# Attention and feed-forward on one core: two silu calls moved into the same beat

## The chip, the core and the metric

The kernel runs on one core of a Trainium2 chip. A core has a matrix engine (TensorE, PE in the profile, with its weight loads as PEld), a vector engine (VectorE, DVE), a scalar engine that evaluates functions from tables (ScalarE, ACT), a general engine (GpSimd, POOL), and queues that start transfers (SyncE, SP, and the queue of POOL). Each engine works through its own list of instructions in order and waits on semaphores for the others.

The metric is the device time of one execution in microseconds, as the median of several executions. A profile describes one execution, which has its own time.

## The reference, cut to what matters

A layer of cross-attention is followed by a feed-forward layer with quantized weights and activations. There are 2048 latent tokens of width 256, and 1601 context tokens; keys and values come from both.

```python
x = x + _L0_xattn_ref(ctx_1024, _layernorm(x), mask, ...)   # 4 heads of 64, rmsnorm on q and k, softmax
x = x + _L0_ffn_ref(_layernorm(x), w1, conv_w, conv_b, w2)

def _L0_ffn_ref(x, w1, conv_w, conv_b, w2):
    h = bit_linear(x, w1)                    # 256 -> 1024, activations and weights rounded
    h = depthwise_conv1d(h^T, conv_w, conv_b)^T   # three taps along the tokens
    h = jax.nn.silu(h)
    return bit_linear(h, w2)                 # 1024 -> 256, the scale is a maximum over the 1024
```

## The kernel before, in words

**The attention loop.** The 2048 queries are cut into four blocks of 512, and the four heads into two pairs. A block and a pair make a unit, so there are eight units. The keys make 29 blocks of 128. A unit goes over them in ten beats: nine of three key blocks and a last one of two. The loop (`for k in range(len(units) * NB)`) thus has 80 beats. In beat k it emits, in this order: the running sums of the exponentials of this beat (`add_up`: one or two of three by an accumulating transfer from the queue of POOL, into `acc` and `acd`, the rest by VectorE into `vec`); the score matmuls `st` of beat k+1, each followed by its exponential `pt` on ScalarE; the matmuls `ot` of this beat (`attend`); and then whatever is planned for the beat under the four marks FRONT, MID, END and LATE.

**Buffers that matter here.** The scores go into a pool of three banks of PSUM (`ps_b`, the tag "big"). The same three banks also serve the first feed-forward matmul `ph`, the look at the next unit's scores `sa`, and the product `py`. The exponentials have six buffers `pt` in SBUF. The feed-forward tiles `pre` and `h` have three and two buffers, `side` has one.

**The feed-forward inside the loop.** The tokens are cut into eight groups of 256, and the 1024 hidden channels into chunks of 128. A slot s handles two chunks of one group, so a group has four slots. Groups 0 to 3 run inside the loop, and the first slot of group 4 too: 17 slots. They start at beats 30, 48, 56, 68 and 76 (the list in front of the loop), one slot every two beats (`pace=2`). All steps of a slot are planned by `feed_forward` under LATE, after everything else of their beat. For a slot at beat t: `hidden` (matmul `ph`) and `dequantize` (DVE, `h`) at t-1; `taps` at t (three ACT instructions into `side`, two DVE into `pre`); `last_tap` at t+1 (POOL and DVE, ending in `pre`); `silu` at t+3 (one ACT instruction of 128x512, from `pre` into half of a tile `t`). `magnitudes` takes the maxima of a whole tile `t` one beat after the odd slot's silu. The scales, the rounding and the second matmul `py` of the group follow.

**The order of the work.** The wrapper `InOrder` keeps the instructions of each engine in program order. So the plan is the order on each engine. On ScalarE a silu comes behind the exponentials of its beat and ahead of those of the next. Exponential and silu use different function tables, and the compiler puts a table load (ACT_TABLE_LOAD) where the function changes: a silu among exponentials has one in front of it and one behind it.

**After the loop** (the tail) the last unit is divided and projected, and the rest of the feed-forward runs at its own pace, slot by slot (`tick`), with no exponentials. The program also holds a second copy of the whole layer, behind a test; its instructions are not in the profile.

All the instructions recorded through the wrapper carry line 170 in the profile, so tiles, not lines, tell them apart.

Of the kernel before, what the change touches and what calls it, by code (L numbers as in the profile page):

```python
# [29 lines left out]
def layer(  # L30
# [253 lines left out]
    with tc.tile_pool(name="pro", bufs=1, side="right") as pro, tc.tile_pool(  # L284
# [4 lines left out]
        for a in range(0, NX, 512):  # L289
            n = min(512, NX - a)  # L290
# [303 lines left out]
    def at(k, call, when):  # L594

        plan.setdefault((k, when), []).append(call)
# [32 lines left out]
    with att:  # L629
# [284 lines left out]
        def magnitudes(g, i):  # L914
            b = groups_[g]
            m = fp.tile([P, G], F32, tag="m", name="m", bufs=2)
            vector.tensor_reduce(m, b["t"][i], AX.X, ALU.max, apply_absolute_value=True)
            if i:
                vector.tensor_tensor(m, m, b["m"], ALU.max)
            b["m"] = m  # L920
# [24 lines left out]
        def rounding(g, i, tokens=slice(0, G)):  # L945
            b = groups_[g]
            t = b["t"][i][:, tokens, :]
            vector.tensor_tensor(
                t, t, b["tb"][:, tokens].unsqueeze(2).to_broadcast(list(t.shape)), ALU.mult
            )  # L950
            if "hq" not in b:
                b["hq"] = fp.tile([P, G, NH], BF16, tag="hq", name="hq", bufs=1)
            vector.tensor_scalar(
                b["hq"][:, tokens, ts(i, NC2)], t, MAGIC, -MAGIC, ALU.add, ALU.add
            )
# [20 lines left out]
        def end_product(g, i):  # L976
            product(g, i)
            outputs.append((g, i))
            if not where["later"]:
                output(*outputs.pop())  # L980

        def feed_forward(g, k, slots, pace=2):

            for n in range(slots):
                s, t = g * NP + n, k + n * pace
                for m, call in (
                    (-1, hidden), (-1, dequantize), (0, taps), (1, last_tap), (3, silu),
                ):
                    at(t + m, lambda call=call, s=s: call(s), LATE)
                if n % 2:  # L990
                    at(t + 4, lambda n=n: magnitudes(g, n // 2), LATE)
            if slots < NP:
                return
            t = k + NP * pace
            for m, call in (
                (3, columns), (3, scales), (5, scales_spread), (5, lambda g: rounding(g, 0)),
                (6, lambda g: rounding(g, 1)), (7, lambda g: end_product(g, 0)),
                (7, lambda g: end_product(g, 1)),
            ):
                at(t + m, lambda call=call: call(g), LATE)  # L1000
# [16 lines left out]
        for g, k in enumerate((30, 48, 56, 68)):  # L1017
            feed_forward(g, k, NP)
        feed_forward(4, 76, 1)
        at(NB * len(units) - 6, lambda: diagonals(0), LATE)  # L1020
        at(NB * len(units) - 2, lambda: diagonals(1), LATE)
# [125 lines left out]
        slots = list(range(4 * NP + 1, NG * NP))  # L1147
# [105 lines left out]
```

## Time and profile before

| what | value |
|---|---|
| time, median of 3 executions | 685.49 us (684.77 to 688.87) |
| the profiled execution, its own time | 688.55 us |
| its span in the profile | 686.7 us |
| mean granted TensorE clock | 0.972 |
| PE, DVE, ACT, POOL busy | 629.2, 464.1, 423.8, 276.6 us |
| first silu, last silu of the loop | 306.2 us, 591.9 us |

The profiled execution is one of the slower ones: it took 688.55 us, of which 686.7 us lie in the span and 1.85 us around it. Busy time of PE is modelled from the starts of its pipelined matmuls. In the rows below, a time in brackets is how long the engine sat idle ahead of the row, and the arrow names what it waited for; "issue" means nothing that the profile can name.

### The profile page before, as it was taken

Reading aid. Unit: us, or ns where it says so; the run is one execution under the profiler, and the core shown is the slowest. Engines: PE = TensorE matmul, PEld = TensorE weight load, DVE = VectorE, ACT = ScalarE, POOL = GpSimd, SP = SyncE. Lnnn points to the kernel's source line nnn. Section 1 sums busy time; section 2 is a strip of 40 time slices with the busy share of each in tenths; the row PEclk is TensorE's granted clock in tenths of the full one; section 3 lists DMA queues with packets and bytes.
Section 4 is the critical chain, followed back from the end, with each engine's and each line's share of the span. In section 5 each row is a group of like instructions: output and inputs, shape, how many; then the busy total and the mean of one; then the engine's idle time right before and its main releaser. Section 6 shows DMA issues by size and latency. Waiting matters only on the chain. (4 is left out here: it accounts for less than half of the span.)

```text
span 686.7 us, 8000 instructions
## 1 busy us (share of the span) xinstructions
PE 629.2 (92%) x2796; PEld 266.3 (39%) x2796; DVE 464.1 (68%) x770; ACT 423.8 (62%) x535; POOL 276.6 (40%) x331
## 2 busy tenths in 40 slices
PE   4999898999999999999999999998899999857754
PEld 2555563333333333333334333332333333345542
DVE  3658774332832766596378779757966797897885
ACT  1656556554556445669945469998765789545540
POOL 2656673221221234244245433425354446742330
PEclk9999999999999999999999999999999999997975
DMA  7600003685878674478849447693564576100001
GB/s 241 170 0 0 1 1 92 128 161 111 167 140 183 128 148 93 93 154 152 185 96 172 101 107 154 125 182 94 107 123 92 132 138 114 31 0 16 16 16 36
DMA packets 32220, 72.12 MB, mean 105 GB/s; under 512 B 7531, under 2 KB 16940, under 8 KB 32172
## 3 DMA queue, kind: packets, MB, share of 16 engines
q0 software_dynamic: 16560, 60.30, 43.3%
q1 hardware_dynamic: 14524, 10.45, 5.1%
q10 hardware_dynamic: 1088, 0.79, 0.4%
q8 instruction: 24, 0.39, 0.2%
q14 instruction: 24, 0.20, 0.1%
HBM read 9.13 MB, written 2.10 MB: 16 GB/s over the span
## 5 line engine op out<-in xcount | busy, mean ns | idle before, releaser
L170 ACT ACTIVATE pt<-st,bias 128x1024 f32<-128x1024 f32 x232 | 242.8, 1112 | 123.1 <-issue 64.6
L170 PE MATMUL st<-q_un,kT 64*128 64x512 f32 x928 | 223.7, 611 | 4.7 <-DVE res L170 1.8
L170 PE MATMUL ot<-pt,v_sb 128*64 128x512 f32 x928 | 216.6, 600 | 0.0
L170 DVE TENSOR_TENSOR vec<-vec,pt 128x1024 f32<-128x1024 f32 x107 | 136.7, 1278 | 40.2 <-ACT pt L170 36.3
L170 PEld LDWEIGHTS st<-q_un,kT 64*128 64x128 f32 x928 | 83.0, 187 | 124.8 <-issue 91.3
L170 PEld LDWEIGHTS ot<-pt,v_sb 128*64 128x64 f32 x928 | 60.2, 136 | 136.7 <-issue 130.4
L170 POOL DMA_DIRECT2D acd<-pt x54 | 44.9, 831 | 127.9 <-ACT pt L170 61.4
L170 POOL DMA_DIRECT2D acc<-pt x61 | 52.7, 865 | 69.4 <-ACT pt L170 51.7
L170 POOL TENSOR_TENSOR pre<-pre,side 128x512 f32<-128x512 f32 (+1 forms) x32 | 38.3, 1196 | 62.3 <-DVE pre L170 51.4
L170 ACT ACT_TABLE_LOAD x34 | 43.6, 1283 | 16.6 <-DMA lb<-in_L_xattn_ln_l_b_dram 7.4
L170 PE MATMUL kv<-wkv_sb,feat 128*128 128x512 f32 (+1 forms) x116 | 52.9, 599 | 0.0
L170 POOL TENSOR_TENSOR ss<-ss,neg_half 128x8 f32<-128x8 f32 (+1 forms) x23 | 39.1, 1702 | 1.9
L170 ACT ACTIVATE t<-pre 128x512 f32<-128x512 f32 (+1 forms) x32 | 29.7, 928 | 11.8 <-POOL pre L170 11.6
L170 POOL TENSOR_SCALAR cm<-ones,units 128x128 f32<-128x128 f32 x16 | 11.8, 739 | 61.4 <-DVE units L170 57.9
L170 DVE COPY oT<-ot 128x512 f32<-128x512 f32 x8 | 5.5, 691 | 44.6 <-PE ot L170 44.6
L170 DVE TENSOR_REDUCE ss<-sq 128x8 f32<-128x512 f32 (+1 forms) x23 | 15.5, 672 | 29.0 <-ACT sq L170 28.9
L170 DVE TENSOR_TENSOR h<-ph,ib_all 128x516 f32<-128x516 f32 x32 | 21.9, 686 | 19.0 <-PE ph L170 18.6
L170 PE MATMUL ph<-h,dg 128*128 128x256 f32 x90 | 25.8, 428 | 7.4 <-DVE h L170 7.4
L170 DVE RECIPROCAL r<-dn 128x512 f32<-128x512 f32 (+1 forms) x11 | 27.3, 2478 | 5.7 <-PE dn L170 5.7
L170 PEld LDWEIGHTS kv<-wkv_sb,feat 128*128 128x128 f32 (+1 forms) x116 | 21.2, 192 | 21.9 <-issue 20.9
L170 ACT ACTIVATE side<-h,cw_sb 128x256 f32<-128x256 f32 x66 | 29.6, 506 | 0.0
L170 PE MATMUL py<-w2T,hq 128*128 128x256 bf16 x128 | 20.8, 317 | 7.2 <-DVE hq L170 7.2
(129 smaller groups left out, 708.9 us busy)
## 6 DMA issues: line engine op xcount, KB each, us to landing
acc<-pt POOLq DMA_DIRECT2D x61, 512.0 KB, 5.1
acd<-pt POOLq DMA_DIRECT2D x54, 512.0 KB, 4.8
tok<-in_x_dram SPq DMA_DIRECT2D x4, 512.0 KB, 6.1
w_sb<-in_L_ffn_w_dram SPq DMA_DIRECT2D x4, 512.0 KB, 5.3
q_un<-in_x_dram SPq DMA_DIRECT2D x4, 512.0 KB, 3.9
out_dram<-res SPq DMA_DIRECT2D x16, 128.0 KB, 1.7
tok<-in_ctx_dram SPq DMA_DIRECT2D x3, 512.0 KB, 4.7
wkv_sb<-in_L_xattn_W_kv_dram ACTq DMA_DIRECT2D x1, 512.0 KB, 7.2
```

The source lines that it names most:

```text
L170: return tc.keep_in_program_order(getattr(self.engine, name)(*args, **kwargs))
```

## The change

The silu of an even slot is planned two beats later (`pace` is 2), at the beat of the odd slot that follows it. The two silus then stand one behind the other on ScalarE. The last slot, which is alone in its call (`slots == 1`), keeps its place. Nothing else is edited.

```diff
             for n in range(slots):
                 s, t = g * NP + n, k + n * pace
+
+                last = 3 if n % 2 or slots == 1 else 3 + pace
                 for m, call in (
-                    (-1, hidden), (-1, dequantize), (0, taps), (1, last_tap), (3, silu),
+                    (-1, hidden), (-1, dequantize), (0, taps), (1, last_tap), (last, silu),
                 ):
                     at(t + m, lambda call=call, s=s: call(s), LATE)
                 if n % 2:
                     at(t + 4, lambda n=n: magnitudes(g, n // 2), LATE)
```

For group 0 the silus stood at beats 33, 35, 37 and 39, and now stand at 35, 35, 39 and 39. For the four full groups together, the pairs come at beats 35, 39, 53, 57, 61, 65, 73 and 77; the single one of slot 16 stays at 79, the last beat.

## The prediction

> **What bounds the kernel now.** I read the shares of the page first, then the groups of ScalarE with shapes kept apart, then the timelines of TensorE and ScalarE side by side through the loop, and last the weight loads at the loop's end. From the page and the groups by shape:
>
> ```profile
> PE 629.2 (92%) x2796; PEld 266.3 (39%) x2796; DVE 464.1 (68%) x770; ACT 423.8 (62%) x535; POOL 276.6 (40%) x331
> ...
> L170 ACT ACT_TABLE_LOAD x34 | 43.6, 1283 | 16.6 <-DMA lb<-in_L_xattn_ln_l_b_dram 7.4
> L170 ACT ACTIVATE t<-pre 128x512 f32<-128x512 f32 x17 | 19.5, 1150 | 0.2
> ```
>
> TensorE is the busy engine. The 17 silus of the loop pay for 34 table loads, two each. That is ScalarE's time; what it is worth is seen from TensorE. Its timeline in a stretch with feed-forward slots, a silu every second beat, and then the only gaps of about a microsecond or more after the first silu and before the tail:
>
> ```profile
> 315.15 2.79 PE L170 MATMUL ot<-pt,v_sb 128*64 128x512 f32 x12
> 317.88 0.62 PE L170 MATMUL ph<-xq_all,w1T 128*128 128x258 bf16 x4
> 318.42 2.85 PE L170 MATMUL st<-q_un,kT 64*128 64x512 f32 x12
> 321.20 2.79 PE L170 MATMUL ot<-pt,v_sb 128*64 128x512 f32 x12
> 323.93 2.85 PE L170 MATMUL st<-q_un,kT 64*128 64x512 f32 x12
> ...
> 478.73 1.13 PE L170 MATMUL st<-q_un,kT 64*128 64x512 f32 x4 [1.09 <-DVE h L170]
> 480.73 1.08 PE L170 MATMUL dn<-vec,ones 128*64 128x512 f32 x4 [0.87 <-DVE vec L170]
> ...
> 494.90 3.45 PE L170 MATMUL st<-q_un,kT 64*128 64x512 f32 x8 [1.79 <-DVE res L170]
> ```
>
> Each row begins where the one above ends: a beat is 2.78 us of scores and 2.73 of products, plus 0.54 where `ph` lies between. No bracket stands there, although ScalarE changes tables. The gaps that exist were released by VectorE. Gaps released by an exponential (ACT pt) in the loop after the first silu are two, 0.41 us each, at 405.77 and 537.64; neither follows a silu.
>
> **Part 1: sixteen table loads go.** Eight even slots lose their own pair of loads; the built program shows two silus between one pair, eight times, and the single last one: 18 loads for 34. By the row, 16 x 1.283 = 20.5 us of ScalarE. The Trainium skill ("ScalarE: Activation LUTs", section "What ACT_TABLE_LOAD costs") counts a drain of about 1.38 us with every switch, 2.66 in all, which would make it 16 x 2.66 = 42.6 us. The timeline of ScalarE has no such drain:
>
> ```profile
> 313.61 3.12 ACT L170 ACTIVATE pt<-st,bias 128x1024 f32<-128x1024 f32 x3
> 316.75 1.28 ACT L170 ACT_TABLE_LOAD   x1
> 318.04 1.14 ACT L170 ACTIVATE t<-pre 128x512 f32<-128x512 f32 x1
> 319.63 1.28 ACT L170 ACT_TABLE_LOAD   x1 [0.46 <-issue]
> 320.93 3.12 ACT L170 ACTIVATE pt<-st,bias 128x1024 f32<-128x1024 f32 x3
> ```
>
> The exponentials end at 316.73, the load starts at 316.75 and ends 0.01 before the silu. I take 20.5. On TensorE's path it is worth nothing by either figure, since no matmul waits behind these loads: the first exponential above ends at 322.04, and its score bank is wanted at 323.93. The cover is this slack of 1.89 us; without it each load pair would cost up to 2.57. Where a silu leaves its even beat, ScalarE is earlier and then waits for TensorE's next scores, a `pt` buffer held by a transfer, or the copy `tb`.
>
> **Part 2: the second silu of a pair.** It takes 1.15 us alone; three exponentials take 3.12 where one takes 1.11, so the next in a row costs 0.11 less: 1.04. At eight beats the exponentials behind it come up to 1.04 us later. Queued behind it on ScalarE are the load, the three exponentials, and the three `side` instructions of the next slot; TensorE waits for the first by a score bank, VectorE and POOL by `pt` and `side`. The wait of the load (0.46 in the row above) absorbs part. Pair by pair, from this trace:
>
> - Beat 35 (316.75): 1.04 - 0.46 = 0.58 later. The bank is free at 322.62, wanted at 323.93: nothing.
> - Beat 39 (338.39): no wait ahead of the load, so exponentials start at 343.18 instead of 342.14. The matmul `sa` wants the first one's bank at 344.21, and it now ends at 344.29; two banks later the lag is about the same. A stall of 0.1 to 0.2 with the 0.06 us from an exponential's end to a weight load: I take 0.2.
> - Beats 53 and 57: 0.3 and 0.6 later, wanted 1.3 us or more after: nothing.
> - Beat 61 (475.71): 1.04 later, ending 481.6 for the first; its bank is wanted at 484.31. The gaps at 478.73 and 494.90 hang on VectorE, which works without a break from 475.72 to 495. It was started by `tb` from TensorE's `tpb`, not by a silu: nothing, and nothing gained.
> - Beats 65 and 73: 0.1 and 0.6 later, 1.2 us of slack or more: nothing.
> - Beat 77: below.
>
> `magnitudes` on VectorE waits for the second silu. It starts 0.7 us or more after the silu's new end, except at beat 40, where it slips 0.6 and VectorE then idles 2.35 anyway. The `pre` buffer of an even slot is held two beats longer, so the fourth slot's `taps` want a buffer that is free only after the pair; they stand behind `magnitudes` of the same pair on VectorE, so this wait is never the later one. No transfer and no instruction on POOL or SP is moved. For a transfer into `acc` or `acd` the exponential comes up to 1.04 later, or 1.3 earlier; its `pt` buffer has six turns, and the ones that ScalarE waits for (471.60, 578.33) were issued late by POOL behind other work.
>
> **The loop's end.** There the cover is gone. ScalarE from the last transfer it waits for, then TensorE's weight loads for the last two blocks:
>
> ```profile
> 575.53 1.28 ACT L170 ACT_TABLE_LOAD   x1 [0.47 <-DMA acd<-pt]
> 576.83 1.11 ACT L170 ACTIVATE pt<-st,bias 128x1024 f32<-128x1024 f32 x1
> 578.33 2.12 ACT L170 ACTIVATE pt<-st,bias 128x1024 f32<-128x1024 f32 x2 [0.38 <-DMA acc<-pt]
> ...
> 584.66 1.28 ACT L170 ACT_TABLE_LOAD   x1
> 585.96 1.16 ACT L170 ACTIVATE t<-pre 128x512 f32<-128x512 f32 x1
> 587.13 1.28 ACT L170 ACT_TABLE_LOAD   x1
> 588.42 2.12 ACT L170 ACTIVATE pt<-st,bias 128x1024 f32<-128x1024 f32 x2
> ```
>
> ```profile
> 589.59 0.20 PEld L170 LDWEIGHTS ot<-pt,v_sb 128*64 128x64 f32 x4 [0.86 <-ACT pt L170]
> 590.60 0.20 PEld L170 LDWEIGHTS ot<-pt,v_sb 128*64 128x64 f32 x4 [0.81 <-ACT pt L170]
> ```
>
> From 578.33 ScalarE runs without a pause to 590.5, and the last two products start 0.06 us after their exponentials. A second silu at 587.0 puts the exponentials at 589.46 and the products at 590.63 and 591.64: +1.04 us. Earlier, the lost silu at 572.61 lets the row at 576.83 start at 575.53, but the next waits for the transfer that lands just before 578.33, and that one was issued behind POOL's `dg`: nothing of it arrives. Behind the last product stand `oT`, `dn`, the division and the whole tail, a chain on VectorE and TensorE: all of it moves by 1.04.
>
> **The sum.** 688.55 (span 686.7 and 1.85 around it) + 1.04 + 0.2 = 689.8 for an execution like the profiled one. That one lies 3.06 above the median of the runs, so on the median: 685.49 + 1.24 = 686.7 us, 0.2% more. About 1% (6.9 us) is what a measurement of this kernel can tell from no change.
>
> **Bounds of the unknown.** The second silu can cost from nothing at the end (if the transfer before 578.33 lands 1.3 earlier) to 1.15. Beat 39 lies between 0 and 0.4. The clock of TensorE: before the gap at 494.90 the profile grants full clock, at 495.3 half for 3.4 us, and eight score matmuls take 3.45 instead of 1.99. The Trainium skill ("TensorE: Matmul & The Clock Gate", section "What's actually happening") lets the clock fall after an idle window of about 3.4 us; by that rule a new gap of 1.04 costs no clock, by the row a gap of 1.79 already cost 1.46. Mine is nearer to the gaps of 1.09 and 0.87 at 478 to 481, after which the clock stayed full; I take 0 and keep 1.7 for the range. The tail's own half-clock stretches (from 618.2) may shift either way by as much.
>
> **Rivals.**
>
> *A, forecast, 0.62:* the freed table time lies under TensorE, and the second silu shows at the loop's end: 686.7.
>
> *B, the freed time is worth something, 0.22.* For it: ScalarE is busy 44.6 of 50 us from 300 to 350. Against: TensorE has no gap there. If the transfer before 578.33 comes earlier with the rest, the end slip vanishes (1.24 - 1.04), and both gaps of 0.41 go: 685.49 + 0.2 - 0.82 = 684.9. Faster by over 1% would need 6.9 us, more than all gaps listed.
>
> *C, a half-clock window, 0.10:* the new idle 1.04 and the 0.43 ahead of `dn` fall into one window: 686.7 + 1.7 = 688.4.
>
> *D, slower, 0.06: the score banks.* If the exponentials behind a pair come more than about 1.9 us later than now, the slack at beat 35, the next scores wait for a bank at every pair. By my count they come 0.58 to 1.04 later. If each pair instead passes a whole silu to TensorE: 8 x 1.04 = 8.3, 693.8 us.
>
> **How the numbers follow.** A, B and C are within 1%, save small parts of B and C: same 0.91, faster 0.03, slower 0.06. The range takes in A, B and C with the 1 us or so by which a median of three can stray (the runs of before span 4.1): 684.0 to 689.4.
>
> **What would show it.** In the profile after: 18 table loads (23.1 us), ScalarE busy near 403, PE still without brackets around the pairs at beats 35 to 73, save some 0.2 near 344; the last two `ot` weight loads 1.0 us later than the products ahead of them allow, waiting for ACT pt; the tail as long as before. I am wrong if TensorE shows gaps of ACT pt behind several pairs, if `magnitudes` or `taps` begin to wait for ACT t with TensorE waiting behind them, or if the gaps at 478 to 495 shrink.

## The result

The changed kernel takes 688.36 us, the kernel before 686.83 us in the same comparison (medians of 22 executions each). The ratio is 1.0020, with a 95% interval of 1.0010 to 1.0029: 0.7 to 2.0 us slower, a small loss, but clear of noise. The forecast was +1.24 us on the median of before. That median itself stands 1.34 us higher here than in the three executions shown ahead of the prediction.

The page of the changed kernel, its first part; then from its groups of ScalarE by shape, with the first of them as it was before (busy time and mean, then the idle time just before and what ended it):

```profile
PE 629.2 (92%) x2796; PEld 265.9 (39%) x2796; DVE 464.4 (68%) x770; ACT 401.7 (59%) x519; POOL 276.6 (40%) x331
```

```profile
L170 ACT ACTIVATE pt<-st,bias 128x1024 f32<-128x1024 f32 x232 | 242.8, 1112 | 123.1 <-issue 64.6 <-PE st L170 43.8 <-DMA acc<-pt 7.7
```

```profile
L170 ACT ACTIVATE pt<-st,bias 128x1024 f32<-128x1024 f32 x232 | 243.0, 1112 | 153.5 <-issue 68.1 <-PE st L170 59.0 <-DMA acc<-pt 16.0
...
L170 ACT ACT_TABLE_LOAD x18 | 23.1, 1283 | 7.6 <-DMA lb<-in_L_xattn_ln_l_b_dram 7.3
L170 ACT ACTIVATE t<-pre 128x512 f32<-128x512 f32 x17 | 17.9, 1152 | 0.1
```

Sixteen loads are gone and ScalarE is busy for 22.1 us less: 20.5 of loads, and 1.6 because two silus in a row overlap a little. TensorE's busy time is the same to the tenth. ScalarE's idle time ahead of the exponentials went from 123.1 to 153.5 us: most of what it saved, it now spends waiting for scores (`PE st`, 43.8 to 59.0) and for `pt` buffers (`acc<-pt`, 7.7 to 16.0).

The stretch at beat 35, with its pair of silus, from the timelines of the changed kernel, ScalarE and then TensorE:

```profile
316.37 1.28 ACT L170 ACT_TABLE_LOAD   x1
317.67 2.10 ACT L170 ACTIVATE t<-pre 128x512 f32<-128x512 f32 x2
319.78 1.28 ACT L170 ACT_TABLE_LOAD   x1
321.08 3.12 ACT L170 ACTIVATE pt<-st,bias 128x1024 f32<-128x1024 f32 x3
```

```profile
317.99 2.85 PE L170 MATMUL st<-q_un,kT 64*128 64x512 f32 x12
320.77 2.80 PE L170 MATMUL ot<-pt,v_sb 128*64 128x512 f32 x12
323.49 2.85 PE L170 MATMUL st<-q_un,kT 64*128 64x512 f32 x12
```

The load no longer waits, and TensorE's scores still follow at the old pitch: 323.49 less 317.99 is 5.50 us, against 323.93 less 318.42, 5.51, before. The gaps of the middle of the loop and of its end:

```profile
478.65 1.13 PE L170 MATMUL st<-q_un,kT 64*128 64x512 f32 x4 [1.09 <-DVE h L170]
480.66 1.77 PE L170 MATMUL dn<-vec,ones 128*64 128x512 f32 x4 [0.88 <-DVE vec L170]
...
493.61 3.20 PE L170 MATMUL st<-q_un,kT 64*128 64x512 f32 x12
...
588.70 2.08 PE L170 MATMUL ot<-pt,v_sb 128*64 128x512 f32 x8 [0.81 <-ACT pt L170]
```

The last line is new: TensorE stands 0.81 us in front of the last two products, for an exponential. ScalarE at that place, and the weight loads of the last two blocks:

```profile
576.43 2.12 ACT L170 ACTIVATE pt<-st,bias 128x1024 f32<-128x1024 f32 x2 [1.51 <-DMA acc<-pt]
...
582.77 1.28 ACT L170 ACT_TABLE_LOAD   x1
584.07 2.15 ACT L170 ACTIVATE t<-pre 128x512 f32<-128x512 f32 x2
586.23 1.28 ACT L170 ACT_TABLE_LOAD   x1
587.53 2.12 ACT L170 ACTIVATE pt<-st,bias 128x1024 f32<-128x1024 f32 x2
```

```profile
588.70 0.20 PEld L170 LDWEIGHTS ot<-pt,v_sb 128*64 128x64 f32 x4 [1.69 <-ACT pt L170]
589.70 0.20 PEld L170 LDWEIGHTS ot<-pt,v_sb 128*64 128x64 f32 x4 [0.81 <-ACT pt L170]
```

The gap at 494.90 of the profile before is missing here, though nothing of the change is near it. That is a matter of the clock, and an experiment below was made for it. For the rest I compare stretches between the starts of the same matmuls, since the spans of two profiles differ by more than the change does. The marks are the `dn` of units 2, 3, 5 and 6 and the last one; `dn` adds up the exponentials of a unit, as the sum that it is divided by.

| stretch in us between starts of `dn` | before | changed |
|---|---|---|
| 296.98 to 353.72 (beats 35 and 39) | 56.74 | 57.09 |
| 353.72 to 480.73 (beats 53 and 57) | 127.01 | 127.02 |
| 480.73 to 552.72 (beats 61 and 65) | 71.99 | 70.33 |
| 552.72 to 592.47 (beats 73 and 77) | 39.75 | 40.58 |

The first row has +0.35, the last +0.83. Together they make 1.18 us of the 1.5 us between the medians. The third row, shorter by 1.66, is the clock again. The tail, from the last `dn` to the end, takes 94.2 us in both profiles, at a mean granted clock of 0.82. Over all profiles below it takes 92.8 to 95.6 us, and 94.6 in a second profile of the kernel before: one execution's tail moves by more than the change is worth, so small differences are read from the stretches.

### The profile page after: what moved, and what is told of

It is laid out like the page before. It is cut to its first block, busy times and chain, and to the rows that moved or that the text cites. A ratio compares the mean times of both kernels' runs of the same rounds, so it can differ in the third digit from the quotient of the medians.

```text
span 685.8 us, 7990 instructions
## 1 busy us (share of the span) xinstructions
PE 629.2 (92%) x2796; PEld 265.9 (39%) x2796; DVE 464.4 (68%) x770; ACT 401.7 (59%) x519; POOL 276.6 (40%) x331
## 5 line engine op out<-in xcount | busy, mean ns | idle before, releaser
L170 ACT ACTIVATE pt<-st,bias 128x1024 f32<-128x1024 f32 x232 | 243.0, 1112 | 153.5 <-issue 68.1
L170 PEld LDWEIGHTS st<-q_un,kT 64*128 64x128 f32 x928 | 82.5, 186 | 123.1 <-issue 89.9
L170 ACT ACTIVATE t<-pre 128x512 f32<-128x512 f32 (+1 forms) x32 | 28.1, 930 | 11.7 <-POOL pre L170 11.6
L170 ACT ACT_TABLE_LOAD x18 | 23.1, 1283 | 7.6 <-DMA lb<-in_L_xattn_ln_l_b_dram 7.3
```

Of the source, the lines that this page charges most:

```text
L170: return tc.keep_in_program_order(getattr(self.engine, name)(*args, **kwargs))
```

## The experiments

All ratios are to the kernel before, from executions on the same chip as the run. The stretches are named by their order in the table above, first to fourth.

**Which pairs cost.** Leave the last pair apart:

```diff
-                last = 3 if n % 2 or slots == 1 else 3 + pace
+                last = 3 if n % 2 or slots == 1 or s == 14 else 3 + pace
```

> The changed kernel, but the even silu of the last pair (slot 14) stays in its own beat 75, so beat 77 has one silu; 20 table loads. My theory: the stall ahead of the last two products (0.81 us in the changed kernel) is gone, TensorE stands at the end of the loop 0.83 us earlier against the middle of the loop than in the changed kernel, and only the slip of beat 39 (about 0.35 us) is left: ratio to before near 1.0005. Rival, a cost spread over all pairs: seven eighths of it stay, ratio 1.0015 or more. Rival, the difference is the clock's phase: the stall's going does not matter, ratio anywhere within 0.2% of 1.

Measured: 0.9998 (0.9983 to 1.0012). The first stretch has 57.08, the fourth 39.62, so the slip of beat 39 is there and the one at the end is gone. The ratio alone could not tell the 0.35 us from zero; the trace does.

Leave the second pair apart as well:

```diff
-                last = 3 if n % 2 or slots == 1 else 3 + pace
+                last = 3 if n % 2 or slots == 1 or s in (2, 14) else 3 + pace
```

> As the first, with the even silu of the second pair (slot 2) left in its own beat 37 as well, so that beats 37 and 39 are as before; 22 table loads, six pairs left. My theory: both stalls are gone, TensorE's gaps are those of the kernel before, ratio 1.000: the twelve loads that are saved buy nothing. Rival, the freed time is worth something: 0.1% faster or better. Rival, every pair costs: ratio 1.0012 or more.

Measured: 0.9999 (0.9990 to 1.0008). The first stretch is 56.73 and the fourth 39.61: both slips are gone, and the six pairs left, with 22 loads for 34, neither cost nor gain.

**The loads without the move.** Even silus stay in their beats, but as exponentials, so that no load is needed:

```diff
-            scalar.activation(t.rearrange("p t c -> p c t"), chunk.pop(s)["pre"], AF.Silu)
+            scalar.activation(
+                t.rearrange("p t c -> p c t"), chunk.pop(s)["pre"], AF.Silu if s % 2 or s == 16 else AF.Exp
+            )
```

> The kernel before, with the silu of every even slot in the loop computed as an exponential, which leaves that part of the result out: it stays in its own beat and needs no table load, so 18 loads stand where 34 did and no silu is moved. It takes the loads away without the move. My theory: the loads lie under TensorE, the last pair of beats is as before, ratio 1.000, TensorE's gaps as before. Rival, the freed time is worth something: up to 1 us faster, with the two gaps of 0.41 us or those of 478 to 495 smaller.

Measured: 0.9997 (0.9989 to 1.0004). Its groups of ScalarE show the same 18 loads as the changed kernel, and nearly the same idle time ahead of the exponentials:

```profile
L170 ACT ACTIVATE pt<-st,bias 128x1024 f32<-128x1024 f32 x232 | 243.2, 1113 | 149.1 <-issue 70.8 <-PE st L170 53.1 <-DMA acc<-pt 17.2
...
L170 ACT ACT_TABLE_LOAD x18 | 23.1, 1283 | 9.5 <-DMA lb<-in_L_xattn_ln_l_b_dram 7.3 <-issue 2.0
```

The gaps of 0.41 us are still there, and those of 1.09 and 0.88. Taken alone, 20.5 us of table loads are worth at most 0.8 us by the interval, and the stretches put it at 0.1 us (39.62 for 39.75 in the fourth). Rival B's gaps do not hang on table loads.

**The last pair, one silu more.** The disputed cost doubled:

```diff
-            scalar.activation(t.rearrange("p t c -> p c t"), chunk.pop(s)["pre"], AF.Silu)
+            for _ in range(2 if s == 15 else 1):
+                scalar.activation(t.rearrange("p t c -> p c t"), chunk[s]["pre"], AF.Silu)
+            chunk.pop(s)
```

> The changed kernel with the silu of slot 15, the last of the pair at beat 77, computed twice in a row: one more ScalarE instruction of 1.04 us ahead of the last exponentials. My theory: all of it is paid, the stall ahead of the last two products grows from 0.81 to 1.85 us, the time by 1.04 us over the changed kernel (ratio to before about 1.0035). Rival, the end has slack or the tail takes it back: no change against the changed kernel.

Measured: 1.0054 (1.0036 to 1.0073). The fourth stretch grows from 40.58 to 41.79. Three silus take 3.32 us where two take 2.15, so the extra one costs 1.17 and not 1.04; it writes the same tile as the one before it. The timelines of this run, TensorE's end and ScalarE's silus:

```profile
589.51 2.08 PE L170 MATMUL ot<-pt,v_sb 128*64 128x512 f32 x8 [2.01 <-ACT pt L170]
```

```profile
583.71 3.32 ACT L170 ACTIVATE t<-pre 128x512 f32<-128x512 f32 x3
```

The stall grew by 1.20, from 0.81 to 2.01: at the loop's end ScalarE's time is passed on in full. By the first and the fourth stretch this run is 2.4 us over the kernel before, a ratio of 1.0035, just under the interval that the executions gave. The profile shows one of the two fastest of its eight executions: these took 687.0 us at a granted clock of 0.98, the other six 690.1 to 692.4 at 0.967 to 0.973. Its tail is the shortest of all profiles, 92.8 us at 0.87. What makes the six longer still, no trace shows, so only the stall is taken from this run.

**The slack of the score banks.** The same doubling at the seven other pairs, with the last pair as in the change:

```diff
-            scalar.activation(t.rearrange("p t c -> p c t"), chunk.pop(s)["pre"], AF.Silu)
+            for _ in range(2 if s % 2 and s < 15 else 1):
+                scalar.activation(t.rearrange("p t c -> p c t"), chunk[s]["pre"], AF.Silu)
+            chunk.pop(s)
```

> The changed kernel with the second silu of each of the seven pairs at beats 35 to 73 computed twice, which puts their exponentials about another 1.1 us later; the pair at beat 77 stays as it is. It tries the slack of the score banks. My theory: at beat 35 the first exponential now ends 0.2 us before its bank is wanted, at beats 53 to 73 0.2 us or more before: nothing; at beat 39 the whole extra is paid, about 1.1 us more ahead of and in the matmuls sa and st (0.35 in the changed kernel, some 1.45 here); the stall at the loop's end stays near 0.8. Ratio to before 1.0035. Rival, the score banks are at their limit at every pair: 7 x 1.1 = 7.7 us more, ratio 1.013.

Measured: 1.0005 (0.9993 to 1.0016); my number, 1.0035, was too high. The first stretch is 58.53, another 1.44 over the changed kernel. Of this, 1.17 comes at beat 39, near the 1.1 expected, and 0.27 at beat 35, where I expected nothing. The score matmuls behind the pair of beat 35 in this run:

```profile
323.01 3.11 PE L170 MATMUL st<-q_un,kT 64*128 64x512 f32 x12
```

In the changed kernel the same row takes 2.85 (323.49 above). The first bank was free in time, as counted; the second and the third were not. Beat 73 loses 0.17 in the same way, and the second stretch (127.07) 0.05. So the slack is there, but smaller than my count of the first bank says. Rival D, which has every pair pass on a whole silu, is out. But the fourth stretch is 39.97, with beat 73 in it, where the changed kernel has 40.58: the slip at the end has vanished, without an edit there. The cause that the traces point to is a transfer. On POOL, the six `dg` (tiles of tap weights for the tail) ran faster in this run, and the transfers queued behind them left earlier, counted from the `dn` of unit 6: `acd` by 1.04 us, `acc` by 0.21. The timeline of POOL, first the changed kernel, then this run:

```profile
563.35 5.80 POOL L170 TENSOR_SCALAR dg<-ident,cw_sb 128x128 f32<-128x128 f32 x6
569.11 0.88 POOL L170 DMA_DIRECT2D acd<-pt  x1
569.69 1.20 POOL L170 DMA_DIRECT2D acc<-pt  x1
```

```profile
564.33 4.76 POOL L170 TENSOR_SCALAR dg<-ident,cw_sb 128x128 f32<-128x128 f32 x6
569.04 0.87 POOL L170 DMA_DIRECT2D acd<-pt  x1
570.45 0.86 POOL L170 DMA_DIRECT2D acc<-pt  x1 [0.54 <-ACT side L170]
```

Counted from that `dn` (550.99 and 551.96), the exponential that waits for `acc` starts at 25.44 in the changed kernel (576.43) and at 24.53 here (576.49). This is rival B's mechanism, a transfer that comes early enough to swallow the slip. Why `dg` ran faster was not tried. By the two stretches this run should still be 2.0 us over before; the executions show 1.1 at most. In its profile the tail is 1.3 us shorter than in that of before (93.0 for 94.2); whether this holds for its other executions is not on record, so the difference stays open.

**The transfer behind the slip.** So the next run moved `dg` itself, and no silu:

```diff
-        at(NB * len(units) - 6, lambda: diagonals(0), LATE)
+        at(NB * len(units) - 4, lambda: diagonals(0), LATE)
```

> The changed kernel with the six instructions dg on POOL (5.8 us) planned at beat 76 instead of 74, so that the transfers acd and acc of beats 74 and 75 are no longer issued behind them; no silu is touched. It tries what makes the loop's end depend on ScalarE. My theory: the exponentials that waited for the transfer at 576.43 wait for scores instead, ScalarE is 1.5 us or more earlier from there, the stall of 0.81 us ahead of the last two products is gone, and of the change only the 0.35 us of beat 39 are left: ratio to before 1.0005. Rival, ScalarE's own work between 578 and 590 us is the limit whatever comes before it: the stall stays near 0.8, ratio 1.002.

Measured: 1.0002 (0.9987 to 1.0017), and the fourth stretch 39.85 for 40.58. ScalarE of this run, with all eight pairs in place, and its last twenty products; then the same products in the kernel before:

```profile
575.72 3.13 ACT L170 ACTIVATE pt<-st,bias 128x1024 f32<-128x1024 f32 x3 [2.44 <-PE st L170]
578.72 1.31 ACT L170 ACTIVATE side<-h,cw_sb 128x256 f32<-128x256 f32 x3
581.22 3.12 ACT L170 ACTIVATE pt<-st,bias 128x1024 f32<-128x1024 f32 x3 [1.19 <-issue]
...
585.66 2.10 ACT L170 ACTIVATE t<-pre 128x512 f32<-128x512 f32 x2
```

```profile
587.41 4.91 PE L170 MATMUL ot<-pt,v_sb 128*64 128x512 f32 x20
```

```profile
586.82 4.86 PE L170 MATMUL ot<-pt,v_sb 128*64 128x512 f32 x20
```

The exponentials wait for scores and not for a transfer, ScalarE stands idle for 1.19 us ahead of the pair, and the products take what they took before; the 0.35 of beat 39 stays (57.09 in the first stretch). Of the slip of 0.83, this move takes away 0.73: it hung on the transfer, held up by POOL's `dg`, that kept a `pt` buffer. The end is not without a wait, neither here nor in the kernel before: in the next experiment the same twenty products take 4.51. So the pair may still cost up to 0.4 us of what `dg` moved alone would gain; `dg` moved with the silus apart was not run.

**The gap at 494.90, and the clock.** The three vector instructions of `compare`, a test on the denominators, one beat later, on the kernel before:

```diff
-                at(k + 3, lambda: compare(u, box["r"]), END)
+                at(k + 4, lambda: compare(u, box["r"]), END)
```

> The kernel before, its silus as they were, with the three vector instructions of compare (1.8 us) planned one beat later. It tries whether the gap of 1.79 us at 494.90 hangs on VectorE's work ahead of res and not on ScalarE. My theory: res starts 1.8 us earlier and the gap is gone, 1 to 1.8 us less time, ratio 0.998; where the half clock fell just before the gap it was already part of it, so less than 1.8 on the mean. Rival, something else holds the product banks there: ratio 1.000. Rival, the three instructions do harm in the next beat: 1.001 or more.

Measured: 0.9970 (0.9958 to 0.9983). The third stretch is 68.57. VectorE of this run, then POOL and TensorE at its end:

```profile
492.43 0.87 DVE L170 SCALAR_TENSOR_TENSOR res<-py,am,q_un 128x256 f32<-128x256 f32 x2
493.21 0.48 DVE L170 SCALAR_TENSOR_TENSOR pre<-h,cw_sb,pre 128x256 f32<-128x256 f32 x1
493.61 3.43 DVE L170 TENSOR_TENSOR vec<-vec,pt 128x1024 f32<-128x1024 f32 x2
496.96 0.95 DVE L170 TENSOR_SCALAR within<-r 128x512 bf16<-128x512 f32 x1
```

```profile
559.73 5.68 POOL L170 TENSOR_SCALAR dg<-ident,cw_sb 128x128 f32<-128x128 f32 x6
```

```profile
583.24 4.51 PE L170 MATMUL ot<-pt,v_sb 128*64 128x512 f32 x20
```

`res`, which reads the product `py` and so frees its bank for the next scores, starts at 492.43 instead of 494.37. The gap hung on VectorE, as the prediction said; no table load touched it. The fourth stretch is shorter too, 39.40 for 39.75: `dg` starts 10.6 us after the `dn` of unit 6, for 12.4 before, no exponential waits for a transfer any more, and the last twenty products run without a wait. This fits the run before: the same transfer, here earlier through an edit that touches neither it nor a silu.

The same edit with six pairs of silus:

```diff
-                at(k + 3, lambda: compare(u, box["r"]), END)
+                at(k + 4, lambda: compare(u, box["r"]), END)
...
-                    (-1, hidden), (-1, dequantize), (0, taps), (1, last_tap), (3, silu),
+                    (-1, hidden), (-1, dequantize), (0, taps), (1, last_tap), (last, silu),
```

where `last` is that of the second experiment.

> The same move of compare on the kernel with six pairs of silus (all but those at beats 39 and 77, 22 table loads). My theory: as with the silus apart, ratio 0.998, since the twelve loads are worth nothing on TensorE's path. Rival, with VectorE out of the way ScalarE's load begins to matter: 0.05% or more below the run with the silus apart.

Measured: 0.9984 (0.9973 to 0.9995); the third stretch is 68.57 again and the fourth 39.41, for 39.40 without pairs. The second is 127.19 for 127.01, but 0.16 of this is lost near 372 us, 40 us ahead of its first pair. The median stands 1.2 us above that of `compare` with the silus apart (686.75 and 685.57), in intervals that overlap. The loads still buy nothing.

The kernel before once more, unchanged:

> The kernel before, unchanged, for a second profile of it. My theory: the gaps of TensorE are the same to 0.1 us, but the stretch of half clock of 3.4 us between 478 and 499 us lies elsewhere or is missing[...]; where it lies near 480 the time from there to 550 us is about 1.7 us shorter than in the first profile. Rival, the half clock at 495.3 belongs to the kernel before and that at 480.9 to the changed one: it lies at 495 again.

Measured: 0.9998 (0.9984 to 1.0012). TensorE in this second profile of the kernel before:

```profile
479.78 1.98 PE L170 MATMUL dn<-vec,ones 128*64 128x512 f32 x4 [0.87 <-DVE vec L170]
481.49 3.63 PE L170 MATMUL ot<-pt,v_sb 128*64 128x512 f32 x12
...
492.71 3.23 PE L170 MATMUL st<-q_un,kT 64*128 64x512 f32 x12
```

Here the half clock falls at 479.8, not at 495.3 (the granted clock is 0.53 from 479.8 to 483.4, and `dn` takes 1.98 for 1.08), and the gap ahead of `st` is gone. The fourth stretch is 39.82 in this profile, 39.75 in the first. And the run with `dg` moved, which has all the pairs, has it at 495.8:

```profile
495.49 3.53 PE L170 MATMUL st<-q_un,kT 64*128 64x512 f32 x8 [1.82 <-DVE res L170]
```

So the place of the half clock goes with the execution and not with the kernel. At 480 it costs nothing, as TensorE would have waited for `res` anyway: 70.34 us for the third stretch, the same as in the run with the even silus as exponentials, which has no half clock there. At 495 it costs 1.66: 71.99 in the first profile of before and 72.01 with `dg` moved.

**All that helped together**: seven pairs, `dg` at beat 76, `compare` one beat later.

```diff
-                at(k + 3, lambda: compare(u, box["r"]), END)
+                at(k + 4, lambda: compare(u, box["r"]), END)
...
-                last = 3 if n % 2 or slots == 1 else 3 + pace
+                last = 3 if n % 2 or slots == 1 or s == 2 else 3 + pace
...
-        at(NB * len(units) - 6, lambda: diagonals(0), LATE)
+        at(NB * len(units) - 4, lambda: diagonals(0), LATE)
```

(The diff is against the changed kernel.)

> The changed kernel with the pair at beat 39 left apart (seven pairs, 20 loads), dg at beat 76, and compare one beat later. My theory: no stall is left that a silu makes, and the gap ahead of res is gone as in the run with compare alone: ratio 0.997, the same as that run, since the fourteen loads themselves buy nothing. Rival, with those stalls out of the way the ScalarE time that is saved shows: 0.995 or less.

Measured: 0.9980 (0.9969 to 0.9991). The fourth stretch is 40.39, longer than the 39.40 of `compare` alone: TensorE waits 0.99 us ahead of the last `dn`, for VectorE's `oT`, where 0.42 is usual, and the last twenty products take 4.92 again. VectorE has no pause there: three of its sums `vec`, from 574.50, take 5.25 us, where they take 3.88 in the run with `compare` alone (from 574.15). Whether `dg` at its new place, beside these sums, is the cause was not tried. The kernel with `compare` alone, its silus apart, has the lowest ratio of the study, 1.2 to 2.9 us below the kernel before by its interval; this run's interval overlaps with it, so adding the pairs and the move of `dg` gained nothing that can be told.

## Why the prediction was right

- **What bounds the kernel**: TensorE's chain, with the table loads beneath it. Held. Loads gone without the move: 0.9997 (0.9989 to 1.0004). Moved at the six pairs with slack: 0.9999 (0.9990 to 1.0008).
- **The cost of a load**: 1.283 us, with no drain beside it. Held; the 18 loads measure 1283 ns, and ScalarE's busy time fell by 16 of these and the overlap of the silus.
- **Beat 39**: mechanism right, term undersized, 0.35 us for 0.2 (0.1 to 0.2 was the count). I let only the first bank's lag count and wrote that two banks later it is about the same. In the trace all three banks wait, and the score matmuls go at the exponentials' pitch of 1.00 us instead of their own 0.93. The weight loads of the changed kernel there:

```profile
343.84 0.30 PEld L170 LDWEIGHTS sa<-q_un,kT 64*128 64x128 f32 x4 [0.87 <-ACT pt L170]
344.84 0.30 PEld L170 LDWEIGHTS st<-q_un,kT 64*128 64x128 f32 x4 [0.70 <-ACT pt L170]
345.85 0.30 PEld L170 LDWEIGHTS st<-q_un,kT 64*128 64x128 f32 x4 [0.70 <-ACT pt L170]
```

- **The loop's end**: mechanism right, term oversized. 1.04 forecast; 0.83 over the profile of before (0.76 over its second one), 0.96 over the run that differs only in the last pair (40.58 less 39.62). The second silu adds 0.99 there (2.15 for 1.16), and the exponential behind the transfer starts 0.17 earlier, 25.44 us after the `dn` of unit 6 for 25.61. Shown from both sides: one silu less takes the slip away, one more adds 1.20. What could take it away was rightly named, the transfer behind `dg`: with `dg` moved, 0.73 of it is gone.
- **The sum**: 1.18 in the stretches for 1.24 forecast. That it is so close is luck in part: 0.15 too little at beat 39 and 0.21 too much at the end nearly cancel. The 686.7 us itself was 1.7 too low, since the three executions it started from put the median of before 1.34 too low.
- **The other pairs**: nothing, as counted. With one more silu each, beat 35 loses 0.27 and beat 73 0.17: again the later banks, where my count looked at the first.
- **The rivals**: B's transfer exists, and swallowed the slip in one run of an experiment, but not in the changed kernel. C did not come: the granted clock of the changed kernel is 1.00 from 550.99 to 591.57, the slip included. D's banks had their slack, except at beat 39.
- **The clock**: I wrote that a gap of 1.79 us "already cost 1.46". The gap alone does not do it. The run with the even silus as exponentials has the same gap and its score matmuls at full speed:

```profile
495.51 1.99 PE L170 MATMUL st<-q_un,kT 64*128 64x512 f32 x8 [1.79 <-DVE res L170]
```

- **A sign that misled**: I had written that I would be wrong if the gaps at 478 to 495 shrank. The one at 494.90 did, from 1.79 to about 0.3 within the row at 493.61. The second profile of before shows the same without the change (3.23 for the row at 492.71).

## What to carry to other kernels

Before table loads are saved by batching, look at whether anyone waits behind them: 20.5 us of ScalarE's time were worth nothing, because at these places TensorE did not wait for ScalarE. Batching makes the engine's longest stretch longer while its sum gets shorter, and it is the longest stretch that must fit into the tightest slack; here two places of eight had less than the silu that was added, and these two decided the sign. Count the slack for every buffer of a pool, not for the first alone. Leave such places out of the pattern, or find what uses up their slack, which may be a transfer queued behind other work on a third engine.

## What the runs showed of the hardware that was not expected

The stretch of half clock of 3.4 us in the middle of the loop moves from execution to execution of one and the same kernel, and in five of the twelve profiles there is none near these gaps (granted clock 1.00 from 476 to 500 us). At one place it costs 1.66 us and at another nothing, since the time is waited out anyway. Two single profiles of kernels that differ by 1.2 us in their other stretches can so stand in the wrong order, as these did: a span of 685.8 us for the slower, 686.7 for the faster.

Six instructions `dg` on POOL of the same shape took 5.80 us in the changed kernel, 4.76 in the run with doubled silus, and 9.01 at their later place. What sets this was not tried.
